# Layer 0 of a four-layer graph network: aggregate then project, or project then gather by seven products

## The chip, the cores and the metric

The kernel runs on one core of a Trainium2 chip. A core has a matrix engine (TensorE, called PE in the profile, with PEld for its weight loads), a vector engine (DVE), a scalar engine (ACT), a general engine (GpSimd, called POOL) and a queue engine (SyncE, called SP) that here issues every DMA. They run side by side and wait for each other through semaphores. The working memory is SBUF, matrix products land in PSUM. The metric is the time of one execution on the device in microseconds (us), as a median of several runs; lower is better.

## The reference

There are 64 graphs (B) of 256 nodes (N) with 512 features (F) and a dense 256x256 adjacency each. Four layers follow one another, each of the form x = x + layer(relu(layernorm(x)), adj). All is float32.

```
h = max(layernorm(x), 0)
# layer 0: attention
Wh = h @ W
e  = leaky_relu(Wh @ a[:512] + (Wh @ a[512:]).T, 0.2)
att = softmax(where(adj > 0.5, e, -9e15), axis=1)      # over the rows
x = x + elu(att @ Wh)
# layer 1: x += relu(dh * (adj + I) * dh @ h @ K1 + bias)
# layer 2: x += relu((adj @ h) @ K2) * mask
# layer 3: x += relu(concat(h, adj @ h / deg) @ W3.T)
```

Layer 0 is where the change lies: att @ (h @ W) can be computed in either order, and the logits Wh @ a need either Wh or the vectors W @ a.

## The kernel before, in words

**Tiles.** A graph's x is one tile `xs` of 128 partitions with two halves of 256 nodes, held from its load to its store. `aT` is the transposed adjacency, `h0` to `h3` are the normalised inputs of the layers, and `e` is the attention of layer 0.

**Products.** A 256x512 by 512x512 product, or a 256x256 by 256x512 one, is split into two by two blocks and done by Winograd's scheme with seven block products rather than eight (`project`, L528). It needs sums of the left blocks (S1 to S4) and of the right blocks (T1, T2, T3, T4N). Three PSUM banks `pz`, `pv`, `py` gather the products; each block is copied out ("snap") or added when its bank is ready, so that a bank is copied between two accumulations into it. `Weighted` (L491) gives the operands for x times a weight: each product has two chunks of 128 in the inner dimension, so 14 matmuls of 128x256. `Gathered` (L506) gives those for adjacency times a feature tile `y`: the inner dimension is one chunk, so 7 matmuls. A weight's blocks and their sums lie in `wb`, and `weight_sums` (L268) forms the sums on POOL.

**Two orders of a layer.** Layers 0 and 1 aggregate first: `aggregate` (L467) multiplies h by the attention or adjacency with 8 plain matmuls of 128x256, its result comes out transposed as the left operand of the projection, and `left_sums` (L453) copies it out of PSUM and forms the left sums. Layers 2 and 3 project first: `turn` (L614) transposes h in 32x32 blocks on DVE, stores it to DRAM as `hd`, loads it back as `hw` by four DMAs that complete the transposition, and forms the left sums on DVE and POOL; `neighbours` (L646) projects into a tile `y`, whose seven blocks get their right sums by `differences` (L257, two on DVE and one on POOL); `block_sums` (L665) forms the left sums of the adjacency on POOL; then a `Gathered` product follows.

**Layer 0 before.** `logit_weights` (L285) computes W a once, broadcast over the partitions, as `wa`. For each graph four DVE instructions (L711) multiply h by `wa` and sum, which gives the logits `lg`. The first set of them is needed along the free dimension: `along` (L363) does this by a DVE transposition, a store and a broadcasting load (in graphs 0 to 2 PE does it). Then ACT forms the leaky sum, DVE masks it and takes the maximum, ACT exponentiates and scales. From graph 2 on, the layer aggregates with e and then projects. Graphs 0 and 1 (`FIRST`) transpose h on PE, project first, and gather with four matmuls of 128x512 (L792), so that the projection does not wait for e.

**What sets the order.** The kernel lists all operations of all graphs with an estimated duration, and a planner in the kernel (`Plan.place`, L74) sorts them into one fixed order for each engine: at each step it takes, for every engine, the operation that can start first, and prefers those with an earlier due time (a graph's due time is 18 us after that of the graph before). Buffers are handed out by this planner too, by tag: a tile waits until one of its tag's buffers is free. The estimates are multiplied by a factor per engine (`STRETCH`, L28), and an operation of PE counts as ready only `SPARE` us (L29) after its inputs. The number of buffers for each tag stands in `buffers` (L910). The chip then follows the order with semaphores.

Of the kernel before, what the change touches and what calls it, by code (L numbers as in the profile page):

```python
# [14 lines left out]
P = 128  # L15
# [10 lines left out]
LAST, LATE = 3, 0.5  # L26

STRETCH = {"DVE": 1.15, "ACT": 1.1, "POOL": 1.1, "PE": 1.0, "DMA": 1.0}  # L28
SPARE = 0.3  # L29
# [124 lines left out]
def kernel(  # L154
# [88 lines left out]
    wa = const.tile([P, 2, F], F32, name="wa")  # L243
    wb = [const.tile([P, 7, FH, OH], F32, name=f"wb{n}") for n in range(5)]

    def spread(to, col):

        nc.tensor.transpose(to, col.to_broadcast([P, P]), ident)
# [23 lines left out]
    def weight(n, w):  # L272

        me = Tiles(f"w{n}", 0.0)
        for at, i, j in ((B11, 0, 0), (B12, 0, 1), (B22, 1, 1), (B21, 1, 0)):
            block = w[i * FH * P : (i + 1) * FH * P, j * OH : (j + 1) * OH].rearrange(
                "(k p) o -> p k o", p=P
            )
            me.op("DMA", 256, lambda g, at=at, block=block: nc.sync.dma_start(
                wb[n][:, at], block), (), [f"=wb{n}.{at}"])  # L280
        if n == 0:
            logit_weights(me)
        weight_sums(me.op, n)

    def logit_weights(me):  # L285
# [28 lines left out]
        for j in range(2):  # L314
            declare(f"pwa{j}", [P, F], "ps")
            for i in range(OC):
                op("PE", 0.9, lambda g, i=i, j=j: nc.tensor.matmul(  # L317
                    g[f"pwa{j}"],
                    lhsT=g["a_cols"][:, j * OC + i : j * OC + i + 1].to_broadcast([P, P]),
                    rhs=g[f"wt{i}"],  # L320
                    start=i == 0,
                    stop=i == OC - 1,
                ), ["a_cols", f"wt{i}"] + ([f"pwa{j}"] if i else []), [f"pwa{j}"])
            op("ACT", 0.59, lambda g, j=j: nc.scalar.copy(wa[:, j, :], g[f"pwa{j}"]),  # L324
               [f"pwa{j}"], [f"=wa{j}"])
# [32 lines left out]
    def graph(b):  # L358
# [147 lines left out]
        class Gathered:  # L506
# [14 lines left out]
            def right(self, g, at, k):  # L521
                return g[self.y][:, at]
# [5 lines left out]
        def project(operands, l, keep, keep_us, total, last, also=[], places=None):  # L528
# [8 lines left out]
            for t in "zyv":  # L537
                declare(f"p{t}{l}", [P, OH], "ps")
# [107 lines left out]
        def neighbours(l, w, by=None):  # L646
# [3 lines left out]
            declare(y, [P, 7, OH], tag="xw")  # L650
# [10 lines left out]
            project([Weighted(f"hw{l}", w)], f"y{l}", keep, 0.38, total, last, also, places=places)  # L661
            differences(op, [("DVE", 0.7), ("DVE", 0.48), ("POOL", 0.9)], lambda g: g[y],
                        lambda i: f"{y}.{i}", dict(urgent=True))

        def block_sums(l, a):  # L665
# [5 lines left out]
                g[aw][:, 0], block(g, 0, 1), block(g, 1, 1), ALU.add), [a, f"h{l}.0"], [f"{aw}.{S1}"])  # L671
# [35 lines left out]
        declare("lg", [P, 2, NC])  # L707
        declare("e", [P, NC, N], tag="mva")
        for j in range(2):
            for c in range(NC):  # L710
                op("DVE", 0.77, lambda g, j=j, c=c: nc.vector.scalar_tensor_tensor(  # L711
                    g["e"].rearrange("p c n -> p (c n)"), g["h0"][:, c, :], 1.0, wa[:, j, :], ALU.mult, ALU.mult,
                    accum_out=g["lg"][:, j, c : c + 1]),
                   [f"h0.{c}", f"=wa{j}"], ["e.0", "e.1", f"lg.{j}{c}"])
        if b < ON_PE:
            declare("pl", [P, N], "ps")
            op("PE", 0.23, lambda g: [
                spread(g["pl"][:, c * P : (c + 1) * P], g["lg"][:, 0, c : c + 1]) for c in range(NC)
            ], ["lg.00", "lg.01", "=ident"], ["pl"])
        else:  # L720
            along("pl", lambda g: g["lg"][:, 0, :], ["lg.00", "lg.01"])
        for c in range(NC):
            op("ACT", 0.47, lambda g, c=c: nc.scalar.activation(
                g["e"][:, c, :], g["pl"], AF.Prelu, bias=g["lg"][:, 1, c : c + 1], alpha=ALPHA),
               ["pl", f"lg.1{c}"], [f"e.{c}"], urgent=True)
# [38 lines left out]
        if b < FIRST:  # L764

            for half in range(2):
                pt = f"pt0_{half}"
                declare(pt, [P, FH, N], "ps")

                def go(g, half=half, pt=pt):  # L770
                    for k in range(FH):
                        for c in range(NC):
                            f0 = (half * FH + k) * P
                            nc.tensor.transpose(
                                g[pt][:, k, c * P : (c + 1) * P], g["h0"][:, c, f0 : f0 + P], ident)

                op("PE", 0.5, go, ["h0.0", "h0.1", "=ident"], [pt])
            together("pt0_0", "pt0_1")
            left_sums("pt0_0", "pt0_1", "xw0")
            declare("wh", [P, NC, O], tag="h")  # L780
            places = {(i, j): (lambda g, i=i, j=j: quarter(g["wh"], i, j), f"wh.{i}{j}")
                      for i, j in PLACE}
            project([Weighted("xw0", 0)], 0, plain_keep, 0.38, plain_total,
                    lambda pz: op("ACT", 0.38, lambda g: nc.scalar.copy(quarter(g["wh"], 1, 0), g[pz]),
                                  [pz], ["wh.10"], urgent=True), places=places)
            for i, piece in ((1, second), (0, third)):
                po = f"po{i}"
                declare(po, [P, O], "ps")

                def go(g, i=i, po=po):  # L790
                    for c in range(NC):
                        nc.tensor.matmul(  # L792
                            g[po],
                            lhsT=g["e"][:, c, i * P : (i + 1) * P],
                            rhs=g["wh"][:, c, :],
                            start=c == 0,
                            stop=c == NC - 1,
                        )

                op("PE", 1.73, go, ["e", "wh.00", "wh.01", "wh.10", "wh.11"], [po])  # L800
                elu0(i, piece[1], lambda g, po=po: g[po], [po],
                     lambda g, i=i: g["xs"][:, i, :], XS[2 * i : 2 * i + 2], O, piece[-1], "ac"[i])
            op("POOL", 0.15, lambda g: nc.gpsimd.memset(g["total1"][:, 1:2], 0.0), (), ["total1.10"])
        else:
            aggregate("h0", "e", 0)
            project([Weighted("xw0", 0)], 0, plain_keep, 0.38, plain_total, lambda _: elu0(*first, "a"))
            elu0(*second, "b")
            elu0(*third, "c")
# [99 lines left out]
    for b in range(B):  # L908
        graph(b)
    buffers = dict(  # L910
        xs=8, a_nat=1, ab=1, aT=7, h=4, mva=5, xw=5, c=2, off=1, junk=1, ex256=2, ex512=2,
        a_rows=1, a_cols=1, turned=1, row=16, hd=8, pl=1, ps=8,
    )
    for tag in ("stats", "total", "mv", "rstd", "nb", "deg", "dh", "rdeg", "lg", "top", "den", "mask"):
        buffers[tag] = 6
# [34 lines left out]
```

## Time and profile before

| | |
|---|---|
| median of 3 runs | 2808.23 us (2808.17 to 2810.1) |
| profiled execution, its own time | 2810.17 us |
| its span, first to last instruction | 2808.4 us |
| PE busy | 2785.2 us, 99% |
| DVE, ACT, POOL busy | 78%, 62%, 47% |
| DMA, mean busy share of 16 engines | 37.0% (its main queue) |

The span lies 1.8 us below the time of the same execution and equals the median to 0.2 us. A busy share is an average over the span. In the groups of instructions, a line shows the busy time, the mean of one instruction and the idle time of the engine just before, with what ended it. Matmuls overlap, so their cost is the distance between their starts rather than the duration shown for one. A float32 matmul appears as two instructions.

### The profile page before, as it was taken

What the parts mean: (1) busy time and instruction counts of PE and PEld (TensorE: products, weight loads), DVE (VectorE), ACT (ScalarE), POOL (GpSimd) and SP (SyncE); (2) the same over time, 40 slices, a digit from 0 to 9 for tenths busy, and PEclk for the clock granted to TensorE, in tenths of its full rate; (3) what the DMA queues carried; (4) which work ended last, traced back from release to release, by engine and by line L of the source; (5) the groups of instructions that cost most, each with busy time, mean ns of one, the idle gap of its engine ahead of it and who ended that gap; (6) DMA issues with size and microseconds to landing.
All of it is one profiled execution on the core that took longest, in us unless ns stands there. A gap on an engine that the chain in (4) does not pass through costs nothing.

```text
span 2808.4 us, 42034 instructions
## 1 busy us (share of the span) xinstructions
PE 2785.2 (99%) x12871; PEld 2439.3 (87%) x12871; DVE 2178.9 (78%) x5367; ACT 1750.9 (62%) x4182; POOL 1332.2 (47%) x2328
## 2 busy tenths in 40 slices
PE   7999999999999999999999999999999999999999
PEld 5888888888888888888888888888888888888887
DVE  7887787787778777877877787778777787778764
ACT  6766665666666666656666666666566666666553
POOL 6654544545444445444454444545444545444442
PEclk9999999999999999999999999999999999999999
DMA  5334433334334243333343343434334433334132
GB/s 178 72 83 97 102 87 85 87 86 96 78 88 108 73 96 98 81 88 87 88 99 75 93 96 80 102 81 96 74 96 91 94 81 94 87 81 89 53 90 69
DMA packets 752044, 251.20 MB, mean 89 GB/s; under 512 B 674756, under 2 KB 702028, under 8 KB 751820
## 3 DMA queue, kind: packets, MB, share of 16 engines
q1 hardware_dynamic: 751820, 248.52, 37.0%
q8 instruction: 103, 1.69, 0.3%
q14 instruction: 121, 0.99, 0.1%
HBM read 147.72 MB, written 100.73 MB: 88 GB/s over the span
## 4 chain that ended last, share of the span: by engine, by line
PE 98%; ACT 0%; DVE 0%; DMA 0%; POOL 0%; SPq 0%; issue 0%; DVEq 0%; ACTq 0%
PE pz L546 31%; PE pzy L546 16%; PE pv L546 16%; PE pt L477 15%; PE pvy L546 8%; PE py L546 8%; PE pyy L546 4%; PE po L792 0%; PE pwa_w L317 0%; DMA a_rows_w<-in_L_gnn_a_dram 0%; DMA wb<-in_L_gnn_kernel_dram 0%; POOL wb L264 0%; ACT h L417 0%; ACT h L438 0%; DVE e L711 0%
## 5 line engine op out<-in xcount | busy, mean ns | idle before, releaser
L546 PE MATMUL pzy<-wb,hw 128*128 128x256 f32 x2048 | 519.5, 379 | 0.0
L546 PE MATMUL pz<-wb,xw 128*128 128x256 f32 x2048 | 513.0, 379 | 1.9 <-ACT wh L585 1.3
L546 PEld LDWEIGHTS pz<-wb,xw 128*128 128x128 f32 x2048 | 387.6, 190 | 56.8 <-POOL wb L264 2.0
L546 PEld LDWEIGHTS pzy<-wb,hw 128*128 128x128 f32 x2048 | 389.1, 190 | 52.9
L438 ACT ACTIVATE h<-xs,nb,rstd 128x512 f32<-128x512 f32 x512 | 401.6, 807 | 28.8 <-POOL nb L435 23.9
L417 ACT ACTIVATE h<-xs,mv 128x512 f32<-128x512 f32 x384 | 274.9, 717 | 18.6 <-POOL mv L414 10.6
L448 POOL TENSOR_TENSOR hw<-hw 128x512 f32<-128x512 f32 x128 | 180.6, 1411 | 201.9 <-DVE hw L444 132.9
L546 PE MATMUL pz<-wb,hw 128*128 128x256 f32 x1024 | 263.0, 379 | 0.6 <-ACT c L640 0.6
L546 PE MATMUL pvy<-wb,hw 128*128 128x256 f32 x1024 | 261.0, 379 | 0.0
L546 PE MATMUL pv<-wb,xw 128*128 128x256 f32 x1024 | 258.6, 379 | 1.7 <-DVE wh L587 1.7
L836 DVE SCALAR_TENSOR_TENSOR xs<-c,xs 128x512 f32<-128x512 f32 (+1 forms) x384 | 238.4, 623 | 6.0
L477 PE MATMUL pt<-ahT,h 128*128 128x256 f32 x1024 | 233.7, 379 | 1.5 <-ACT xw L457 1.5
L477 PE MATMUL pt<-e,h 128*128 128x256 f32 x992 | 227.6, 379 | 2.3 <-ACT e L744 2.3
L448 POOL TENSOR_TENSOR xw<-xw 128x512 f32<-128x512 f32 x128 | 171.6, 1341 | 113.5 <-DVE xw L444 58.4
L477 PEld LDWEIGHTS pt<-ahT,h 128*128 128x128 f32 x1024 | 194.5, 190 | 28.7 <-issue 2.1
L546 PEld LDWEIGHTS pv<-wb,xw 128*128 128x128 f32 x1024 | 194.3, 190 | 28.5 <-DVE wh L587 2.1
L546 PEld LDWEIGHTS pz<-wb,hw 128*128 128x128 f32 x1024 | 194.4, 190 | 27.6 <-ACT c L640 1.2
L546 PEld LDWEIGHTS pvy<-wb,hw 128*128 128x128 f32 x1024 | 194.6, 190 | 26.4
L425 POOL TENSOR_TENSOR rstd<-rstd,minus_half 128x2 f32<-128x2 f32 x256 | 204.2, 797 | 19.8
L711 DVE SCALAR_TENSOR_TENSOR e<-h,wa 128x512 f32<-128x512 f32 x256 | 207.8, 812 | 7.0 <-ACT wa L324 4.5
L477 PEld LDWEIGHTS pt<-e,h 128*128 128x128 f32 x992 | 188.3, 190 | 28.2 <-ACT e L744 2.6
L414 POOL TENSOR_SCALAR mv<-total 128x1 f32<-128x1 f32 x192 | 63.8, 333 | 310.5 <-DVE xs L836 194.9
(136 smaller groups left out, 5758.5 us busy)
## 6 DMA issues: line engine op xcount, KB each, us to landing
hd<-h SPq DMA_DIRECT2D x128, 512.0 KB
hw<-hd SPq DMA_DIRECT2D x512, 128.0 KB
xs<-in_x_dram SPq DMA_DIRECT2D x64, 512.0 KB
out_dram<-xs SPq DMA_DIRECT2D x64, 512.0 KB
ab<-in_adj_dram SPq DMA_DIRECT2D x256, 64.0 KB
a_nat<-in_adj_dram SPq DMA_DIRECT2D x64, 256.0 KB
pl<-dpl SPq DMA_DIRECT2D x61, 128.0 KB
wb<-in_L_gnn_kernel_dram SPq DMA_DIRECT2D x8, 256.0 KB
```

Source lines behind the costliest of these rows:

```text
L414: op("POOL", 0.3, lambda g: nc.gpsimd.tensor_scalar(g[mv][:, 0, 0:1], g[t][:, 0:1], -1.0 / F, None, ALU.mult), [f"{t}.0"], [f"{mv}.m0"])
L417: op("ACT", 1.0, lambda g, c=c: nc.scalar.activation(g[h][:, c, :], g["xs"][:, c, :], AF.Square, bias=g[mv][:, 0, c : c + 1], accum_out=g[ ...
L425: op("POOL", 0.72, lambda g: nc.gpsimd.tensor_tensor(g[rs], g[rs], minus_half, ALU.pow), [rs, "=half"], [rs])
L438: op("ACT", 0.81, lambda g, c=c: nc.scalar.activation(g[h][:, c, :], g["xs"][:, c, :], AF.Relu, bias=g[nb][:, c : c + 1], scale=g[rs][:, c ...
L448: op("POOL", 1.45, lambda g: nc.gpsimd.tensor_tensor(flat(g[xw][:, S4 : S3 + 1]), flat(g[xw][:, A12 : A22 + 1 : A22 - A12]), flat(g[xw][:, ...
L477: nc.tensor.matmul(g[pt][:, kk, :], lhsT=g[h][:, c, k * P : (k + 1) * P], rhs=g[moving][:, c, :], start=(c == 0), stop=(c == NC - 1),)
L546: nc.tensor.matmul(g[t], lhsT=o.left(g, left, k), rhs=o.right(g, right, k), start=start and n == 0, stop=n == len(parts) - 1, skip_group_c ...
L711: op("DVE", 0.77, lambda g, j=j, c=c: nc.vector.scalar_tensor_tensor(g["e"].rearrange("p c n -> p (c n)"), g["h0"][:, c, :], 1.0, wa[:, j, ...
L836: lambda g, kw: nc.vector.scalar_tensor_tensor(to(g), y(g), 0.0, to(g), ALU.max, ALU.add, **kw), y_keys, to_keys,
```

## The change

- Layer 0 now has the form of layers 2 and 3: from graph 2 on, h0 goes through `turn(0)`; graphs 0 and 1 still transpose on PE. Then `neighbours(0, 0)` projects into `y0`, `block_sums(0, "e")` forms the left sums of the attention, and a `Gathered` product follows, in all graphs.
- W's blocks have one more column, W a: in the blocks of the left column of W it is W a[:512], in the right ones W a[512:]. The projection then gives the logits as column 257 of y0's blocks, so its matmuls are 128x257. The four DVE sums and `wa` go. `logit_weights` forms W a by 16 matmuls with two columns each, and four ACT copies put it into `wb0`, before `weight_sums`.
- The right operands y have a tag of their own with 3 buffers. Other buffers: aT 7 to 6, h 4 to 3, xw 5 to 3, c 2 to 3, ex256 2 to 3, ex512 2 to 1.
- The planner's numbers change: DVE 1.15 to 1.1, ACT 1.1 to 1.03, POOL 1.1 to 1.25, SPARE 0.3 to 0.15, and the last 2 graphs rather than 3 come due closer to one another.

```diff
-LAST, LATE = 3, 0.5
-STRETCH = {"DVE": 1.15, "ACT": 1.1, "POOL": 1.1, "PE": 1.0, "DMA": 1.0}
-SPARE = 0.3
+LAST, LATE = 2, 0.5
+STRETCH = {"DVE": 1.1, "ACT": 1.03, "POOL": 1.25, "PE": 1.0, "DMA": 1.0}
+SPARE = 0.15
...
-    wa = const.tile([P, 2, F], F32, name="wa")
-    wb = [const.tile([P, 7, FH, OH], F32, name=f"wb{n}") for n in range(5)]
+    wb = [const.tile([P, 7, FH, OH + (n == 0)], F32, name=f"wb{n}") for n in range(5)]
...
+        declare("pwa", [P, FC, 2], "ps")
+
+        def go(g):
+            for k in range(FC):
+                for i in range(OC):
+                    nc.tensor.matmul(
+                        g["pwa"][:, k, :],
+                        lhsT=g[f"wt{i}"][:, k * P : (k + 1) * P],
+                        rhs=g["a_cols"][:, i::OC],
+                        start=i == 0,
+                        stop=i == OC - 1,
+                    )
+
+        op("PE", 2.5, go, ["a_cols"] + [f"wt{i}" for i in range(OC)], ["pwa"])
+        for (half, j), at in blocks.items():
+            op("ACT", 0.2, lambda g, half=half, j=j, at=at: nc.scalar.copy(
+                wb[0][:, at, :, OH], g["pwa"][:, half * FH : (half + 1) * FH, j]),
+               ["pwa"], [f"=wb0.{at}"])
...
-            declare(y, [P, 7, OH], tag="xw")
+            declare(y, [P, 7, width], tag="y")
...
-        for j in range(2):
-            for c in range(NC):
-                op("DVE", 0.77, lambda g, j=j, c=c: nc.vector.scalar_tensor_tensor(
-                    g["e"].rearrange("p c n -> p (c n)"), g["h0"][:, c, :], 1.0, wa[:, j, :], ALU.mult, ALU.mult,
-                    accum_out=g["lg"][:, j, c : c + 1]),
-                   [f"h0.{c}", f"=wa{j}"], ["e.0", "e.1", f"lg.{j}{c}"])
+        if b < FIRST:
...
+            left_sums("pt0_0", "pt0_1", "xw0")
+        else:
+            turn(0)
+        neighbours(0, 0, x="xw0" if b < FIRST else None, width=OH + 1)
+
+        L1 = lambda g: g["y0"][:, B11 : B21 + 1 : B21 - B11, OH]
...
-            along("pl", lambda g: g["lg"][:, 0, :], ["lg.00", "lg.01"])
+            along("pl", L1, L1_KEYS)
...
-        else:
-            aggregate("h0", "e", 0)
-            project([Weighted("xw0", 0)], 0, plain_keep, 0.38, plain_total, lambda _: elu0(*first, "a"))
-            elu0(*second, "b")
-            elu0(*third, "c")
+        block_sums(0, "e")
+        project([Gathered("e", "aw0", "y0")], 0, plain_keep, 0.38, plain_total, lambda _: elu0(*first, "a"))
+        elu0(*second, "b")
+        elu0(*third, "c")
...
-        xs=8, a_nat=1, ab=1, aT=7, h=4, mva=5, xw=5, c=2, off=1, junk=1, ex256=2, ex512=2,
-        a_rows=1, a_cols=1, turned=1, row=16, hd=8, pl=1, ps=8,
+        xs=8, a_nat=1, ab=1, aT=6, h=3, mva=5, xw=3, c=3, off=1, junk=1, ex256=3, ex512=1,
+        a_rows=1, a_cols=1, turned=1, row=16, hd=8, y=3, pl=1, ps=8,
```

## The prediction, made before the changed kernel had run

> **What bounds the kernel now.** I read first the shares of the page, then the busy time of each engine in three stretches (start, middle, end), then the waits of PE alone, then the groups of instructions that the change touches.
>
> ```profile
> PE 2785.2 (99%) x12871; PEld 2439.3 (87%) x12871; DVE 2178.9 (78%) x5367; ACT 1750.9 (62%) x4182; POOL 1332.2 (47%) x2328
> 0.00:100.00 100.00, 82.50 (x354) 62.29 (x355) 79.45 (x190) 68.23 (x171) 65.54 (x92) 1.00 0.51 144
> 100.00:2790.00 2690.00, 2690.00 (x12463) 2366.50 (x12462) 2093.34 (x5166) 1679.82 (x4006) 1265.97 (x2236) 1.00 0.37 88
> 2790.00:2808.00 18.00, 12.66 (x58) 10.49 (x56) 6.13 (x12) 2.84 (x6) 0.72 (x1) 1.00 0.15 58
> ```
>
> PE is busy for 2690.0 of the 2690 us in the middle. All its idle time, 23.2 us, is 17.5 at the start and 5.3 at the end (plus rounding). So the span is PE's instructions plus those 23 us, and other engines matter only where they make PE wait. Its waits say what the start hangs on: weights from DMA, and e.
>
> ```profile
> PE pw_w L308 <- DMA wb<-in_L_gnn_W_dram: 6.5, 2, 3.8
> PE pt L477 <- ACT e L744: 2.3, 1, 2.3
> 49.61 3.45 PE pt L477 x16
> ```
>
> The last line, of the chain that ended last, gives the price of a product: 16 instructions in 3.45 us are 0.2156 us each. A float32 matmul is two of them, so 128x256 costs 0.431 us (the 379 ns of the groups includes the overlapped drain).
>
> SP, which issues every DMA in order, already stands long in places (total us, times, longest):
>
> ```profile
> SPq L623 <- DVE h L619: 440.4, 92, 19.0
> SPq L628 <- DMA hd<-h: 104.7, 42, 4.7
> ```
>
> The groups that go or are copied (busy us, mean ns, idle before):
>
> ```profile
> L711 DVE SCALAR_TENSOR_TENSOR e<-h,wa 128x512 f32<-128x512 f32 x256 | 207.8, 812 | 7.0 <-ACT wa L324 4.5
> L619 DVE STREAM_TRANSPOSE h<-h 128x512 f32<-128x512 f32 x256 | 173.6, 695 | 11.3 <-ACT h L438 11.3
> L448 POOL TENSOR_TENSOR hw<-hw 128x512 f32<-128x512 f32 x128 | 180.6, 1411 | 201.9 <-DVE hw L444 132.9 <-PE pt L477 22.4 <-PE pz L546 20.4
> L317 PE MATMUL pwa_w<-wt_w,a_cols_w 128*128 128x512 f32 x16 | 9.4, 728 | 0.0
> q1 hardware_dynamic: 751820, 248.52, 37.0%
> ```
>
> **What the Trainium skill says.** "TensorE: Matmul & The Clock Gate", section Back-to-back issue gap: N/2.4 + 2.5 ns, 215.7 ns for 512 columns. Here a 256-column float32 instruction takes 215.6 ns, so it streams 512 steps; one column more should be two steps, 0.83 ns. "SBUF — State Buffer", section Who interferes with whom: a DVE instruction with two SBUF inputs and a GpSimd instruction that reads SBUF exclude each other, while PE and ACT wait on nobody. The trace agrees: L444 takes 601 ns on xw but 449 ns on hw, the same size. "DMA: Bandwidth & Descriptors", Specifications: line rate needs 512 B or more; here 674,756 of 752,044 packets are smaller, and a turn adds such packets.
>
> **The change on PE.** Layer 0 of a graph is now 8 products of 128x256 (aggregate) and 14 (project), 22. Changed: 14 of 128x257 and 7 of 128x256. The changed order shows just this, so the change does what it says. Saved: one product, 431 ns; added: 14 x 2 x 0.83 = 23 ns; net 0.408 us. Graphs 0 and 1 swap four 512-wide products (worth 8) for 7, the same sum. 64 x 0.408 = 26.1 us. All of this is on the engine that sets the end.
> The logit weights: 16 instructions at about 0.43 us (6.9) become 32 with two columns each, bound by their weight load. The nearest rows are the transposes L344 (10 in 1.25 less drain, 0.11 each): 3.5 us. Bounds: 0.025 (the floor for small N in the same page and section) to 0.19 (a weight load), 0.8 to 6.1 us. Saved 3.4 (0.8 to 6.1). PE's work: 2785.2 - 26.1 - 3.4 = 2755.7.
>
> **What moves to other engines, per graph (from graph 2 on).** DVE loses four logit sums (4 x 0.893 with the accumulator's 81 ns) and two left sums (0.42 + 0.60), 4.59; gains two transposes (1.39), two sums of hw (0.97), three totals (1.26), two differences (0.72 + 0.49), 4.83. Net +0.2 on 34.0. ACT: -0.59 - 0.37 + 4 x 0.37 = +0.5. POOL: -1.34 + 1.41 + 0.79 (difference) + 1.78 (block sums) = +2.6 on 20.8, so 54%. At 43.1 us of PE per graph none becomes the bound (DVE about 80%). I cost these at nothing because PE's 43 us hide them; without that cover DVE's 0.2 us would still be only 15 us in all.
> DMA: one store and four loads more per graph, 4096 packets of 128 B and some 256 large ones on 11,750: by packets 37% becomes about 51%. SP: 0.34 + 4 x 0.68 = 3.1 us more of issue per graph, in one queue with inputs, outputs and the logits' row.
>
> **Does PE stay fed?** I added 0.2156 us per instruction along the changed PE order, graphs 12 to 55. From the last z product of y0 to the first product that reads e lie at least 34 us of PE work. The work needed: copy 0.37, transpose 0.23, store to load 2.25, landing at most 6.1 (load at 1199.48, Prelu at 1205.57), Prelu 1.0, minimum 0.81, maximum 0.67, exponentials 1.4, reciprocal 0.15, scaling 1.0, hops about 2: some 16. From layer 0's last z product to layer 1's first: at least 19.4 (before 23.7), needed some 10. From layer 1 to layer 2's first: at least 29.8 (before 37.1), needed some 20: norm and transposes 9, store 4.4 (issued 1180.59, loads 1184.95), loads 2.8 and landing, sums. Buffers: aT 7 to 6; from an aT's last product to the product that needs the next one in its place lie at least 44 us (before 65). So all long waits are covered, with less cover than before. Short ones are tighter: accumulations whose bank is copied between two products have at least three matmuls (1.29 us) between them; 21 pairs stand at this least distance before, 99 after. Needed: 0.21 (PE to ACT, seen at 1196.57), 0.47, 0.2 back, 0.9. A 0.81 us normalisation started just ahead can exceed it by 0.4. I allow 2 us in all for them.
>
> **The start.** Column 257 of W must be there before POOL forms W's sums; before, POOL began at 9.7 us, as soon as W had landed. Now: PE transposes W, four copies (2.4), products (3.5), four small copies (0.8), sums 2.4 + 1.4 + 1.4, done near 21 us. The first projection ends near 25 instead of 32.6, since PE no longer spends 9.4 us on pwa. But then e(0) needs y0 and graph 0's gather stands behind w3's transposes, whose load (SP) is queued behind the store hd(0 of graph 2), itself waiting for h. I get e at 34, w3 at 37, gather done at 41. Graph 2 comes through a turn, with DMA busy 57 to 99% in every 5 us until 50 here: hw near 44. Layer 1 of graph 0 starts near 55 instead of 49.5, with 23 us idle by then, and 25 in all: 7.5 more than now. Bounds: 0 (the turn lands early) and 18.
>
> **Sum.** 2755.7 + 25 + 5.3 + 2 = 2788 against the profile's span of 2808.4. The median is 2808.23, so the span stands for it: 2788, 0.7% faster.
>
> **Rivals.** (A, 0.68) the above, own range 2775 to 2800.
> (B, 0.14) short waits: 99/44 = 2.25 tight pairs a graph, each late by 0.1 us on average, add 14 us: 2802. For it: the smaller margins; against it: no wait of PE at all after 100 us today, with 21 such pairs.
> (C, 0.10) slower: hw of layer 0 lands late. Place: SP issues in order, and stands in waits of up to 19.0 us already (for the transposed h); five more transfers join it. PE stands still at the first product of y0, and every later product with it. Price: 1 us per graph is 62 us; at 0.32 us per graph the gain is gone, above 0.42 it is measurably slower; at 0.7 us, 2831. Against it: x is loaded graphs ahead.
> (D, 0.05) rows of 1028 B cost PE more than 0.83 ns: 21 products x 64 of this kind, so 15 ns each (3.5%) would eat the gain: about 2808. No 257-wide or unaligned operand is in this trace. A gain from it is excluded, since no operand became narrower; I take 0.
> The rest (0.03) is unforeseen, at any of the three.
>
> **How the numbers follow.** Faster: all of A, 0.10 of B, 0.01 of the rest and D: 0.79. Same, within 0.2% (2802.6 to 2813.8; less than that this measurement can't tell): 0.04 of B, 0.03 of D, 0.01: 0.08. Slower: C and what is left, 0.13. The range 2772 to 2811 holds A and B, and most of D; C lies above.
>
> **What would show it.** Right: PE busy near 2756 us; no idle from about 110 us to the last 20; idle of the first 100 us near 25; groups of 128x257 with a mean at most 2 ns above 379; POOL near 54%, DMA near 51%. Wrong: idle of PE spread over the middle, ended by ACT or DVE (B), or by DVE's hw or POOL's hw at y0 (C); fewer PE instructions per us than 4.64 without idle (D); or a start that costs over 18 us more.

## The result, and the profile after

The kernel after takes 2790.0 us (median of 4 runs, 2789.43 to 2790.91); the kernel before took 2808.78 us beside it on the same chip. The ratio is 0.9933, with a 95% interval of 0.9916 to 0.995: 0.7% faster. The profiled execution took 2790.29 us, its span is 2788.5 us, so spans can be set against spans: 2808.4 became 2788.5, 19.9 us less.

The shares of the page and the main DMA queue, kernel after:

```profile
PE 2766.1 (99%) x12775; PEld 2423.6 (87%) x12775; DVE 2217.1 (80%) x5305; ACT 1782.1 (64%) x4318; POOL 1464.1 (53%) x2582
q1 hardware_dynamic: 1018668, 313.56, 48.1%
```

PE has 96 instructions less: 124 fewer in the 62 graphs that aggregated first (22 products became 21), 12 more in the first two, 16 more for W a. Its busy time fell by 19.1 us and its idle time from 23.2 to 22.4 us. POOL went from 47 to 53% and DMA from 37.0 to 48.1%.

The busy time in three stretches, kernel after (the columns are the stretch, its length, then busy us and instructions of PE, PEld, DVE, ACT and POOL, the granted clock, the DMA share and GB/s):

```profile
0.00:100.00 100.00, 84.49 (x369) 69.53 (x370) 74.33 (x172) 63.41 (x173) 66.24 (x97) 0.97 0.76 186
100.00:2770.00 2670.00, 2668.78 (x12351) 2343.47 (x12350) 2136.44 (x5122) 1715.81 (x4141) 1397.10 (x2485) 1.00 0.48 111
2770.00:2789.00 19.00, 12.82 (x59) 10.62 (x57) 6.33 (x13) 2.84 (x6) 0.73 (x1) 0.92 0.15 55
```

The middle is full: 1.2 us of idle in 2670. The other idle time is 15.5 us in the first 100 (17.5 before) and 5.7 at the end (the last stretch ends 0.5 us after the span). The waits of PE over the whole span, the four largest (total us, times, longest); all but 1.2 us of its waiting before the end lies in the first 100 us:

```profile
PE pw_w L307 <- DMA wb<-in_L_gnn_W_dram: 4.4, 3, 3.7
PE pzy L551 <- ACT y L590: 3.3, 5, 1.3
PE pzy L551 <- DMA hw<-hd: 2.2, 1, 2.2
PE pt L482 <- POOL y L263: 2.0, 1, 2.0
```

The load of the transposed h, `hw`, which the change adds to layer 0, makes PE wait once, in graph 2, for 2.2 us, and never again. The same products as 128x256 and as 128x257, from the groups of instructions by shape (busy us, mean ns of one, idle before):

```profile
L551 PE MATMUL pzy<-wb,hw 128*128 128x256 f32 x2048 | 524.8, 379 | 0.5 <-ACT y L590 0.5
L551 PE MATMUL pzy<-wb,hw 128*128 128x257 f32 x992 | 256.6, 381 | 2.2 <-DMA hw<-hd 2.2
```

**The price of a graph.** In the chain of work the order of PE repeats, and so gives an exact period. Before, six graphs take 259.01 us (from 770.44 to 1029.46 us of its chain): 43.17 us each, 100 products of 0.4317. After, 16 graphs lie between these two lines:

```profile
774.88 3.45 PE pt L482 x16
...
1459.24 3.45 PE pt L482 x16
```

684.36 us by 16 is 42.77 us. A graph gained 0.396 us, 64 graphs 25.3 us. The span gained only 19.9. W a gave 2 us more (8.9 us from start to start before, 7.0 now), and idle time fell by 0.8 us, which makes 28. So about 8 us were given back, in PE's busy time; most of them can be seen at the start.

The order in time on PE in the first 68 us, kernel after (start, duration, line, tiles, count, idle before and what ended it):

```profile
10.22 6.99 PE L318 MATMUL pwa_w<-a_cols_w,wt_w 128*128 128x2 f32 x32 [0.26 <-ACT a_cols_w L295]
...
20.60 1.92 PE L551 MATMUL pzy<-wb,xw 128*128 128x257 f32 x4
22.31 1.92 PE L551 MATMUL pyy<-wb,xw 128*128 128x257 f32 x4
...
25.18 1.03 PE L551 MATMUL pzy<-wb,xw 128*128 128x257 f32 x4
...
48.35 1.94 PE L551 MATMUL pzy<-wb,hw 128*128 128x257 f32 x4 [2.20 <-DMA hw<-hd]
...
61.82 5.38 PE L482 MATMUL pt<-ahT,h 128*128 128x256 f32 x16 [2.01 <-POOL y L263]
```

Four instructions of a product take 1.03 us at 25.18, but 1.92 at 20.60 and 22.31 and 1.94 at 48.35; sixteen take 5.38 us at 61.82 instead of 3.62. PE ran at half its rate there, for about 3.4 us each time. From start to start: 20.60 to 24.02 is 1.7 us more than eight instructions of 0.2156, 48.35 to 51.79 again 1.7, 61.82 to 67.03 is 1.8 more than sixteen, and the eight transposes from 18.35 to 20.60 lose about 0.9: 6.1 us of the 8. The kernel before has no such stretch after its logit weights. The other 2 us were not placed.

### The profile page after: what moved, and what is told of

Read it like the earlier page. It is cut to its first block, busy times and chain, and to the rows that moved or that the text cites. A ratio compares the mean times of both kernels' runs of the same rounds, so it can differ in the third digit from the quotient of the medians.

```text
span 2788.5 us, 43020 instructions
## 1 busy us (share of the span) xinstructions
PE 2766.1 (99%) x12775; PEld 2423.6 (87%) x12775; DVE 2217.1 (80%) x5305; ACT 1782.1 (64%) x4318; POOL 1464.1 (53%) x2582
## 3 DMA queue, kind: packets, MB, share of 16 engines
q1 hardware_dynamic: 1018668, 313.56, 48.1%
## 4 chain that ended last, share of the span: by engine, by line
PE 98%; DVE 1%; DMA 0%; SPq 0%; ACT 0%; issue 0%; POOL 0%; DVEq 0%; POOLq 0%; ACTq 0%
PE pz L551 28%; PE pzy L551 24%; PE pv L551 14%; PE pvy L551 12%; PE pt L482 8%; PE py L551 7%; PE pyy L551 6%; PE pwa_w L318 0%; DMA a_rows_w<-in_L_gnn_a_dram 0%; DMA w3n_w<-in_L_gnn_W_dram 0%; DVE e L752 0%; DVE y L263 0%; DVE h L624 0%; SPq L691 0%; DVE y L592 0%
## 5 line engine op out<-in xcount | busy, mean ns | idle before, releaser
L551 PE MATMUL pzy<-wb,hw 128*128 128x257 f32 (+1 forms) x3040 | 772.0, 380 | 2.7 <-DMA hw<-hd 2.2
L551 PE MATMUL pvy<-wb,hw 128*128 128x256 f32 (+1 forms) x1520 | 382.6, 380 | 0.0
L590 ACT COPY y<-pzy 128x256 f32<-128x256 f32 (+1 forms) x512 | 190.7, 372 | 281.7 <-PE pzy L551 232.7
L624 DVE STREAM_TRANSPOSE h<-h 128x512 f32<-128x512 f32 x380 | 257.3, 693 | 36.0 <-ACT h L443 36.0
L551 PE MATMUL pz<-wb,xw 128*128 128x256 f32 x1024 | 263.0, 379 | 0.8 <-DVE c L804 0.5
L263 DVE TENSOR_TENSOR y<-y 128x256 f32<-128x256 f32 (+1 forms) x384 | 231.3, 628 | 7.0
L551 PE MATMUL pz<-y,aw 128*128 128x256 f32 x768 | 228.4, 379 | 0.0
L551 PE MATMUL pv<-y,aw 128*128 128x256 f32 x768 | 228.4, 379 | 0.0
L816 DVE SCALAR_TENSOR_TENSOR xs<-c,xs 128x256 f32<-128x256 f32 (+1 forms) x384 | 221.3, 578 | 3.8
L551 PEld LDWEIGHTS pz<-wb,xw 128*128 128x128 f32 x1024 | 194.0, 190 | 28.5 <-POOL rstd L426 0.9
```

Source lines behind the costliest of these rows:

```text
L263: op(eng, us, lambda g, on=on, to=to, i=i, j=j: on.tensor_tensor(tile(g)[:, to], tile(g)[:, i], tile(g)[:, j], ALU.subtract), [key(n) for ...
L551: nc.tensor.matmul(g[t], lhsT=o.left(g, left, k), rhs=o.right(g, right, k), start=start and n == 0, stop=n == len(parts) - 1, skip_group_c ...
L590: return "ACT", lambda g, to, block: nc.scalar.copy(to, block)
L624: op("DVE", 0.71, lambda g, c=c: nc.vector.transpose(g[h][:, c, :], g[h][:, c, :]), [f"{h}.{c}"], [f"{h}.{c}"])
L816: lambda g, kw: nc.vector.scalar_tensor_tensor(to(g), y(g), 0.0, to(g), ALU.max, ALU.add, **kw), y_keys, to_keys,
```

## The experiments

The theory (T): PE sets the time, a product costs 0.4317 us wherever it stands, and everything that was moved to DVE, ACT, POOL, SP and DMA is hidden. The rivals: short waits at the tight accumulations (B), the turn of layer 0 late (C), the wide rows dear (D), and, since the change has more parts than the new layer 0, that the planner's numbers or the buffers carry the gain. The runs are numbered in their order; e3 was a first form of e7.

One reading serves for all runs. Where PE's order is fixed and every instruction costs the same, lost time shows as missing instructions in a stretch, whether PE stood idle or ran at half rate. The table counts PE's instructions by stretch from the busy time of the engines, and multiplies what is missing by 0.2156 us. Runs e1 and e4 contain 128 more and 16 fewer instructions than after, which is added (27.6 us) or taken off (3.4 us). The last two rows have the kernel before as their base.

| run | 0 to 100 | 100 to 400 | 400 to 2400 | 2400 to 2700 | missing | makes | span longer by |
|---|---|---|---|---|---|---|---|
| after | 369 | 1380 | 9260 | 1391 | | | |
| e1, a product more | 372 | 1345 | 9260 | 1383 | 40 | 8.6 + 27.6 | 36.3 |
| e4, logits on DVE | 329 | 1340 | 9108 | 1359 | 264 | 56.9 - 3.4 | 53.2 |
| e5, DVE + 4 | 339 | 1334 | 9194 | 1379 | 154 | 33.2 | 32.8 |
| e6, DVE + 2 | 351 | 1360 | 9259 | 1390 | 40 | 8.6 | 8.7 |
| e8, planner back | 345 | 1338 | 9254 | 1376 | 87 | 18.8 | 18.3 |
| e10, y in xw | 369 | 1376 | 9260 | 1390 | 5 | 1.1 | 1.0 |
| e11, warm start (without its 20) | 373 | 1380 | 9260 | 1390 | -3 | -0.6 | -0.9 |
| e12, twin turn | 315 | 1376 | 9232 | 1382 | 95 | 20.5 | 20.2 |
| before | 354 | 1392 | 9268 | 1390 | | | |
| e9, before, new numbers | 299 | 1352 | 9268 | 1392 | 93 | 20.1 | 19.8 |

The last two columns agree within 0.5 us in every row, so no loss is hidden after 2700 us and each is placed. Most of it lies in the first 400 us, save in e4 and e5, where the middle loses the most or nearly as much as the start.

### A product more (e1), and wider rows (e2)

```diff
 # e1: project(), first of the seven products
+            if any(isinstance(o, Gathered) for o in operands) and l == 0:
+                product("z", A11, B11, True)
             product("z", A11, B11, True)
 # e2
-    wb = [const.tile([P, 7, FH, OH + (n == 0)], F32, name=f"wb{n}") for n in range(5)]
+    wb = [const.tile([P, 7, FH, OH + 16 * (n == 0)], F32, name=f"wb{n}") for n in range(5)]
...
-        neighbours(0, 0, x="xw0" if b < FIRST else None, width=OH + 1)
+        neighbours(0, 0, x="xw0" if b < FIRST else None, width=OH + 16)
```

> The kernel after, with one redundant product in layer 0 of each graph (the first product of the gather is formed twice, its bank started anew, so that the values stay the same): one 128x256 float32 matmul more per graph, on PE alone. Theory T (PE sets the time, a product costs 0.4317 us, the other engines are hidden): the steady period of a graph goes from 42.77 to 43.20 us, +27.6 us in all, about 2817 to 2818 us. Rival S (from the halved steps on, something beside PE sets the pace, so that PE has slack): +0 to 15 us.

> The kernel after, with 16 extra columns in place of one in layer 0's projection (all hold W a, so the work that counts is the same): 14 matmuls per graph of 128x272 instead of 128x257. Three prices of a column: linear, 0.83 ns per column and instruction, +350 ns per graph, period 43.12 us, about +22 us; the 1.3 ns that the period after shows for column 257, +550 ns, period 43.32, about +35 us; a fixed cost of an odd width or of rows that are not a multiple of 512 B (rival D), period 42.8 to 43.1, that is +0 to 22 us, or less than linear.

**Measured.** e1: 2827.75 us, ratio to before 1.0068 (1.0045 to 1.0091). e2: 2810.87 us, 1.0008 (0.9998 to 1.0019). The chain of e1, three graphs apart:

```profile
702.77 3.45 PE pt L482 x16
...
832.38 3.45 PE pt L482 x16
```

129.61 us by 3 is 43.20 us: one product is worth 0.431 us per graph, as T has it. The total missed T's number by 10 us; the table shows where: 35 instructions are missing between 100 and 400 us and 8 near the end. The planner, given one more product, made an order that loses more there.

e2's chain has 689.73 us for 16 graphs (781.03 to 1470.76): 43.11 us, 336 ns above after. By 15 columns and 28 instructions that is 0.80 ns per column, the linear price, and the whole predicts 21.5 us where the span grew by 20.9. Its group of wide instructions:

```profile
L551 PE MATMUL pzy<-wb,hw 128*128 128x272 f32 x992 | 267.9, 393 | 0.6 <-DMA hw<-hd 0.6
```

**What follows.** Rival S (PE has slack) falls, and so does rival D at the size that would matter: column 257 costs about 1.2 ns an instruction (42.773 less 99 times 0.4317, by 28), of which 0.8 is the column. What the other 0.4 is was not tried.

### The logits back on DVE (e4), and DVE loaded without another order (e5, e6)

```diff
 # e4: layer 0 keeps the new order, products 256 wide
+        for j in range(2):
+            for c in range(NC):
+                op("DVE", 0.77, lambda g, j=j, c=c: nc.vector.scalar_tensor_tensor(
+                    g["sc"], g["h0"][:, c, :], 1.0, wa[:, j, :], ALU.mult, ALU.mult,
+                    accum_out=g["lg"][:, j, c : c + 1]),
+                   [f"h0.{c}", f"=wa{j}"], ["sc", f"lg.{j}{c}"])
...
-        xs=8, a_nat=1, ab=1, aT=6, h=3, mva=5, xw=3, c=3, off=1, junk=1, ex256=3, ex512=1,
+        xs=8, a_nat=1, ab=1, aT=6, h=3, mva=5, xw=3, c=2, off=1, junk=1, ex256=2, ex512=1,
 # e5: two ahead of the mask, one ahead of each transposition of h0;
 # e6: one ahead of the mask, one ahead of one transposition
+    def dead_work(of, n):
+        for _ in range(n):
+            nc.vector.scalar_tensor_tensor(
+                dead, of, 1.0, of, ALU.mult, ALU.mult, accum_out=dead_sum)
```

> The kernel after in its order (project, then gather by seven products), but with the logits as before: four DVE sums of h0 and wa, products 256 wide, W a broadcast by 16 matmuls of 128x512; buffers c and ex256 2 instead of 3. It tells the column from the reordering. Theory T: the reordering alone gives the gain; PE work per graph 42.74 us (99 products of 0.4317), 0.03 us less than after, DVE 3.6 us more per graph (88%), hidden; W a 7 to 9 us on PE; so 2786 to 2794. Rival: without the column DVE's load makes PE wait, idle in the middle, 2800 or more; or the column is what gains, and the period goes back towards 43.17 us.

> The kernel after in its own order and with its own buffers, but each graph has four more DVE instructions that do no useful work (a 128x512 product and sum into a tile that nothing reads): two right before the mask of layer 0, one before each transposition of h0. DVE gets 3.6 us more per graph (four of 0.893 us), as the logit sums cost it, so about 88% busy; the planner does not know of them. The run with DVE logits took 2844 us with many waits of PE of about 0.4 us on copies out of PSUM. If DVE's load is their cause (theory L): PE shows such waits here too, tens of us in all, and the time is 2815 to 2850. If its planned order or its two smaller buffers were the cause (rival O): 2790 to 2796, no idle of PE in the middle.

> As the run with four idle DVE instructions per graph, but with two (one before the mask, one before one of the transpositions; 1.8 us per graph, DVE about 84%). Theory L, a smooth one: a third to a half of the loss of four. Theory L with a threshold: 2790 to 2796 here and the loss only with four. Rival O: 2790 to 2796 in both.

**Measured.** e4: 2844.33 us, 1.0124 (1.0094 to 1.0153), slower than before. e5: 2824.34 us, 1.0054 (1.0032 to 1.0077). e6: 2798.94 us, 0.9966 (0.9951 to 0.9982). The expectation T of e4 failed by 50 us. The stretch from 400 to 2400 us, first of e6, then of e5:

```profile
400.00:2400.00 2000.00, 2000.00 (x9259) 1757.17 (x9258) 1676.13 (x4070) 1296.53 (x3133) 1070.77 (x1875) 1.00 0.50 115
```

```profile
400.00:2400.00 2000.00, 1991.21 (x9194) 1743.05 (x9193) 1742.88 (x4237) 1286.76 (x3111) 1070.76 (x1864) 1.00 0.50 115
```

With DVE busy for 1676 of 2000 us (83.8%) PE loses nothing here; with 1743 (87.1%) it loses 66 instructions, 14 us. The waits of PE in that stretch, e5 and then e4:

```profile
PE pv L558 <- DVE c L655: 8.0, 12, 0.7
PE pz L558 <- DVE c L812: 0.6, 1, 0.6
```

```profile
PE pzy L546 <- ACT y L585: 10.6, 23, 0.5
PE pv L546 <- DVE c L587: 5.5, 23, 0.2
```

These are rival B's waits: a product that waits for its bank to be copied or added out. The counted idle (8.6 and 16.1 us) is less than the missing instructions (14.2 and 32.8 us); a part of each wait probably lies within the modelled ends of the matmuls. In e5 eleven of the twelve waits come 172.2 us apart, one in every four graphs. At two of them, at 1016.79 and 1189.00 us, all four added instructions stand in the 6 us ahead of the late copy, on a DVE that had not paused: at the first since 1004.89 us. In e4 ACT has a wait of its own that after has not:

```profile
ACT c L585 <- DVE xs L817: 58.2, 23, 2.5
```

Its copy into `c` waits for a `c` buffer that DVE's update of x still reads, 2.5 us every second graph, and the copies out of `pzy` stand behind it.

**What follows.** Theory L (DVE's load makes PE wait) holds. Of its two forms neither number came: e6 ends 8.9 us above after, where the threshold allowed 6 and the smooth form asked for 11 or more. In the steady state it looks like a threshold, nothing lost at 84% of DVE and 14 us at 87%; only the first 400 us lose in e6 (38 instructions, 8.2 us). But the share alone does not set it: e4 loses more than e5 at 85.6%, and e5's waits come where its added work bunches. Whether the four instructions, spread out, would cost as much was not tried. For e4 there is the second `c` buffer's loss too, and another order; those two were not separated. What is shown is that the column of logits is no ornament: this build with the seven products, the logits on DVE and one buffer fewer for `c` and for `ex256` is some 35 us slower than before.

### The turn of layer 0 (e7, e12)

```diff
 # e12: the store, and likewise the loads, issued twice, the second into DRAM that nothing reads
 # (e7: each issued twice with the same destination)
-            op("DMA", 512, lambda g: nc.sync.dma_start(
-                g[hd].rearrange("(p x) -> p x", p=P), g[h].rearrange("p c f -> p (c f)")),
+            op("DMA", 512, lambda g: [nc.sync.dma_start(
+                to.rearrange("(p x) -> p x", p=P), g[h].rearrange("p c f -> p (c f)"))
+                for to in [g[hd]] + [hd_twin] * (l == 0)],
```

> The kernel after, but layer 0's store of h and its four loads are issued twice each (5 more DMAs per graph, same data; DMA busy about 60% instead of 48%, SP 3.1 us more issue per graph). The planner does not know of them, the order is that of after. Theory T: DMA and SP have room, no idle of PE in the middle, 2790 within 4 us (the start may lose 1 to 3 us). Rival C (the turn of layer 0 is close to being late): idle of PE at the first product of y0, ended by the load of hw; 1 us per graph is 62 us, so 2820 or more.

> The kernel after, but the store and the four loads of layer 0's h are each followed by a twin with the same source, the same packets and a destination in DRAM that nothing reads, so that no twin waits for its fellow as the second loads did in the run with a doubled turn (there SP waited 626 us for the first loads to land). DMA about 60% busy, SP 3.1 us more issue per graph, order as in after. Theory T: DMA and SP have room, no idle of PE in the middle, 2788 to 2800. Rival C: hw comes late at the first product of y0, 2820 or more.

**Measured.** e7: 3451.2 us, 1.2283 (1.2248 to 1.2319). e12: 2809.46 us, 1.0002 (0.9992 to 1.0011). e3, a first form in which the planner placed the doubled transfers itself, gave no time: its order came to a point where no instruction could start. The waits of SP, which issues the DMAs, in e7:

```profile
SPq L634 <- DMA hw<-hd: 625.8, 248, 6.3
SPq L628 <- DVE h L624: 438.9, 102, 26.8
```

248 is four loads in 62 graphs. The second load writes where the first one writes, so SP stood still until the first had landed, 2.5 us each time, and every input, output and row behind it stood too. The run was meant to double the traffic and instead made SP's queue wait; it says nothing on how near after is to C, but it shows what a late turn would cost: with 10 us of such waits per graph in that queue the kernel is 661 us longer.

e12 doubles the traffic without that wait: SP shows none for `hw` any more. DMA is at 60% from 400 to 2400 us:

```profile
0.00:100.00 100.00, 76.38 (x315) 61.57 (x316) 63.38 (x148) 53.63 (x150) 54.45 (x81) 0.91 0.87 218
100.00:400.00 300.00, 298.09 (x1376) 259.79 (x1374) 243.07 (x584) 202.69 (x493) 172.02 (x299) 1.00 0.54 125
400.00:2400.00 2000.00, 1998.10 (x9232) 1750.56 (x9231) 1614.31 (x3876) 1290.31 (x3127) 1051.03 (x1872) 1.00 0.60 139
```

**What follows.** Neither theory's number came. The steady state has nearly enough room: 28 instructions, 6.0 us over 47 graphs, are lost with a second turn per graph. The start has none: with DMA at 87% in the first 100 us, 54 instructions are missing there, 11.6 us. One turn per graph, as in after, is free in the steady state (PE is busy for 2000.0 of these 2000 us there). That its loads already compete with the weights and the first inputs at the start of after is likely, with DMA at 76% there, but no run has taken the turn out.

### The planner's numbers (e8, e9), and the tag of y (e10)

```diff
 # e8: after with the first of each pair, e9: before with the second
-LAST, LATE = 3, 0.5
-STRETCH = {"DVE": 1.15, "ACT": 1.1, "POOL": 1.1, "PE": 1.0, "DMA": 1.0}
-SPARE = 0.3
+LAST, LATE = 2, 0.5
+STRETCH = {"DVE": 1.1, "ACT": 1.03, "POOL": 1.25, "PE": 1.0, "DMA": 1.0}
+SPARE = 0.15
 # e10
-            declare(y, [P, 7, width], tag="y")
+            declare(y, [P, 7, width], tag="xw")
...
-        xs=8, a_nat=1, ab=1, aT=6, h=3, mva=5, xw=3, c=3, off=1, junk=1, ex256=3, ex512=1,
-        a_rows=1, a_cols=1, turned=1, row=16, hd=8, y=3, pl=1, ps=8,
+        xs=8, a_nat=1, ab=1, aT=6, h=3, mva=5, xw=6, c=3, off=1, junk=1, ex256=3, ex512=1,
+        a_rows=1, a_cols=1, turned=1, row=16, hd=8, pl=1, ps=8,
```

> The kernel after with the planner's numbers of before (1.15, 1.1, 1.1, 0.3, the last 3 graphs closer together) and after's buffers. Theory T: the numbers decide only the order, PE has no idle in the middle either way, 2788 to 2796. Rival: the new numbers carry part of the gain; with the old ones short waits of PE come back, 2796 to 2810.

> The kernel before with only the planner's numbers of after (1.1, 1.03, 1.25, 0.15, the last 2 graphs), its buffers and its layer 0 unchanged. The steady period stays at 43.17 us a graph either way. If the numbers are good for the start by themselves (theory N): idle of PE in the first 100 us falls from 17.5, 2795 to 2805. If they only suit the new order (theory M): the start or short waits get worse, 2810 to 2830. If they are worth nothing to before: 2806 to 2811.

> The kernel after with the right operands y back in the tag of the left sums, which gets 6 buffers (3 and 3 before, so the memory is about the same). This part of the change gives no work away: if PE stays fed, the period is 42.77 us and only the start and the end can move, 2785 to 2805. Rival: y and xw then take each other's buffers and PE waits for a free one, 2810 or more, with idle in the middle.

**Measured.** e10: 2790.97 us, 0.9935 (0.9915 to 0.9955). The other two complete a square:

| | planner's numbers of before | of after |
|---|---|---|
| layer 0 of before | 2808.78 us | e9: 2829.87 us, 1.0073 (1.0053 to 1.0093) |
| layer 0 of after | e8: 2810.55 us, 1.0003 (0.9993 to 1.0013) | 2790.0 us |

The start of e8, and below it that of e9:

```profile
0.00:100.00 100.00, 77.47 (x345) 61.94 (x345) 70.52 (x156) 58.41 (x157) 61.26 (x87) 0.98 0.68 181
100.00:400.00 300.00, 294.12 (x1338) 251.23 (x1338) 236.61 (x573) 196.61 (x480) 164.39 (x289) 1.00 0.43 101
```

```profile
0.00:100.00 100.00, 74.14 (x299) 53.58 (x300) 82.20 (x183) 62.88 (x161) 63.69 (x90) 0.94 0.51 145
100.00:400.00 300.00, 296.11 (x1352) 258.84 (x1351) 226.97 (x575) 189.42 (x459) 141.12 (x252) 0.99 0.34 81
```

**What follows.** The period is 42.77 us in e8 (1172.82 to 1215.59 in its chain) and 43.17 us in e9 (701.47 to 830.98, three graphs): the price of a graph belongs to layer 0's form and not to the planner. The start depends on the planner. With the numbers of before, the new layer 0 loses 66 instructions in the first 400 us and gains nothing in all; with the numbers of after, the old layer 0 loses 95 there. Each set suits the order that it stands with. Theory M is right for e9 and the rival right for e8, though not as it was put: there are no short waits in the middle, the loss is at the two ends. The tag of y's own makes no measurable difference. Two things stay open: which of the planner's numbers it is, since all were changed together, and what the other buffer counts do. They can't carry the gain of 0.396 us a graph, since PE is full in the middle before and after, but they may have a part in the start.

### PE's clock at the start (e11)

```diff
+WARM = 10
...
+        declare("warm", [P, P], "ps")
+        op("PE", 1.5, lambda g: [
+            nc.tensor.matmul(g["warm"], lhsT=ident, rhs=ident, start=True, stop=True) for _ in range(WARM)
+        ], ["=ident"], ["warm"])
```

> The kernel after with ten idle 128x128 float32 matmuls of the identity at the head of PE's order, while PE waits for W; the order of all else is that of after. Theory K (PE's clock, still at half rate, is what made the 32 products of W a take 7.0 us and the first products of the projection 0.43 us an instruction): the transposes of W go at 0.11 us each, the 32 products take 3.5 to 5 us, the first product starts 2 to 3.5 us sooner than 20.6, and the total is 0 to 6 us less. Rival W (the 32 products are set by their weight loads or by the wait for each other): they take 7.0 us as in after, and the total is the same within 2 us, or up to 2 more.

**Measured.** 2788.76 us, 0.9928 (0.9911 to 0.9944). PE's order in time, e11:

```profile
1.34 3.93 PE L295 MATMUL warm_w<-ident 128*128 128x128 f32 x20 [1.34 <-POOL minus_half L253]
...
9.50 5.46 PE L323 MATMUL pwa_w<-a_cols_w,wt_w 128*128 128x2 f32 x32 [0.86 <-ACT a_cols_w L300]
...
18.35 1.92 PE L556 MATMUL pzy<-wb,xw 128*128 128x257 f32 x4
...
47.32 1.11 PE L556 MATMUL pzy<-wb,hw 128*128 128x257 f32 x4 [1.89 <-DMA hw<-hd]
...
60.85 3.69 PE L487 MATMUL pt<-ahT,h 128*128 128x256 f32 x16 [1.87 <-POOL y L264]
```

W a takes 5.46 us instead of 6.99 and the first product starts 2.25 us sooner; the products at 47 and 61 us run at full rate here. Some 6 us of half rate are gone (2.25, and 1.7 and 1.8 at the two places). Yet the product at 47.32 starts only 1.03 us sooner than in after, that at 60.85 only 0.97, and the end comes 0.9 us sooner.

**What follows.** Theory K is right on the cause (the 32 products of W a take about 0.11 us each as long as the clock is up, by the windows below; they come to 5.46 us, above its 3.5 to 5, because the clock falls on the way), and the total lies in its range, but a difference of 1.2 us is within what these medians can tell from nothing (the intervals of the two ratios overlap almost wholly). The order in time suggests why: the product at 47.32 still waits 1.89 us for `hw`, so what was won ahead of it is lost again to other waits. One of them is new: the next `pzy` product waits 1.50 us for ACT at 51.67, where after has no wait. At the start, half rate and idle time take each other's place.

e11 and e10 are no better than after by more than the measurement tells; no run gave a version that clearly beats it.

## Why the prediction was right, and where it was wrong

**PE is the bound and a product costs 0.4317 us: right.** e1 gives 0.431 us per graph for one product, and the middle of after is full (1.2 us idle of 2670). The saving was put at 0.408 us a graph and 26.1 us; measured 0.396 and 25.3. The term that was off is the wide column: 1.67 ns for two instructions was predicted, 2.4 came (e2: 0.80 ns per column is right, the rest was not explained). The 128x257 group's mean is 381 ns, 2 above 379.

**Side engines hidden: right in the steady state, for a reason that was only half said.** POOL 53% (54 predicted), DMA 48.1% (51), DVE 80%. The cover was taken to be PE's 43 us against DVE's 34. e5 and e6 show that the cover of DVE can end far below 100%: at 83.8% it costs nothing, at 87.1% it costs 14 us in the steady state. Rival B's tight pairs are real; e4 and e5 point to the column, which took the four logit sums off DVE, as what keeps them quiet in after. The prediction's sentence that without cover DVE's 0.2 us would be 15 us in all treated DVE's load as time in a queue. It acts as a risk of being late.

**Cover of the turn (rival C): right.** hw made PE wait once. Even a second turn per graph (e12) costs only 6.0 us over 47 graphs, 0.13 us each, less than the 0.32 at which C would have eaten the gain. At the start it costs more: e12 loses 12.5 of its 20 us in the first 400.

**The start: the sum right, its parts wrong.** Predicted were 25 us of idle time in the first 100, and W a at 3.5 us instead of 6.9. Measured: 15.5 us of idle, W a at 7.0 instead of 8.9, and 6.1 us of half rate. Most of W a before, in its order in time on PE:

```profile
11.30 1.92 PE L317 MATMUL pwa_w<-wt_w,a_cols_w 128*128 128x512 f32 x2
...
13.43 6.46 PE L317 MATMUL pwa_w<-wt_w,a_cols_w 128*128 128x512 f32 x12
```

The step that failed is the price of PE's instructions there. For W a before, 0.43 us an instruction was taken, but its first two took 1.71 us, to the next start at 13.01. For a 128x2 product, 0.11 us was taken from transposes that ran at full rate. All products were taken at 0.2156. PE's busy time came out 10.4 us above 2755.7: 1.5 for W a (3.4 saved in the prediction, 1.9 measured), 6.1 of half rate, 0.8 for the columns, and the 2 that were not placed. The idle time came out 9.9 below 32.3 (25, 5.3 and 2). That the two errors cancel to half a microsecond is luck; that they have opposite signs is not wholly. In e11 some 6 us of half rate are taken away and the total falls by 1 us, since waits take their place. The marks of the working were late too: gather done near 46 us, not 41; layer 1 of graph 0 at 61.8, not 55. Half rate does not explain that: in e11, with little of it left, layer 1 still starts at 60.85. Why was not traced.

**What the prediction left out: the planner's numbers.** It followed the changed order and so had their effect within it, but gave them no line of their own. None of its rivals was an order with a bad start, though a start over 18 us worse was among its signs of being wrong. e8 shows that this was as large a term as the saving itself: with the old numbers the same layer 0 is 20.6 us slower, and the gain is gone. e1, e8 and e9 put 7, 14 and 20 us into the first 400 us that no count of operations would give. The prediction read its start off the actual order, and so could come near it.

**The range.** 2788 us against a median of 2790.0; the likeliest case's own range, 2775 to 2800, held it.

## What to carry to other kernels

Where one engine is full, count its instructions: a change of its steady work can be priced to 1 us in 25 from one repeated distance in the chain. Price the start apart, and along the actual order, since there idle time and half rate replace each other and a planner's margins can be worth as much as the whole saving. An engine that is hidden on average can still be late where its work bunches: when work is moved onto or off it, ask what waits right behind that work, not only whether the sum fits.

## What the runs showed of the hardware that was not expected

**PE can fall to half rate while it works without a pause.** In e11 PE enters the 32 products of W a at full rate and falls out of it while it works on them without a pause. The stretches of those instructions alone (PE, PEld, granted clock, DMA share, GB/s):

```profile
9.50:10.50 1.00, 1.00 (x9) 1.00 (x10) 1.00 1.02 138
10.50:11.50 1.00, 1.00 (x10) 1.00 (x9) 0.86 0.71 72
11.50:12.50 1.00, 1.00 (x7) 1.00 (x6) 0.50 0.26 55
```

The granted clock is 1.00, 0.86 and then 0.50, and it stays there to the end of the 32. In after the same 32 products, begun at half rate, did not release it in 6.99 us. After them the first projection begins at half rate in both, e11 and after. The Trainium skill, "TensorE: Matmul & The Clock Gate", section Part 1: The HAM clock gate (the "warmup" mystery), says that the half rate is the default and that some 3.4 us of sustained activity release it; the products at 20.60 to 24.02 us of after agree if one counts from the first product (3.4 us at half rate), for the transposes ahead of it ran slow too. That section names idle time as what brings the half rate back; here PE fell back in the middle of its work. Waits of 0.48, 0.55 and 0.86 us and small transposes stand in the 3.4 us ahead of these products in e11, and may have a part; that the width of two columns is the cause was not tried. In after the granted clock of the records is 1.00 during W a, though each product takes 0.218 us, twice 0.109: the spacing of the instructions is the better witness.

**The length of a gap alone does not say whether the clock falls.** The same page, section Why this matters for your kernels, warns of gaps of more than about 3 us. In after, gaps of 2.01 and 2.20 us were followed by half rate. In before, this one of 2.33 us was not, sixteen instructions in 3.72 us (its order in time on PE):

```profile
64.36 3.72 PE L477 MATMUL pt<-e,h 128*128 128x256 f32 x16 [2.33 <-ACT e L744]
```

In e11 gaps of 1.87 and 1.89 us were not either. In e12 one of 2.21 us was followed by half rate (16 instructions in 5.38 us), and one of 2.28 us was not (four in 1.13 us). The gap of 2.20 us follows 4 us in which products alternate with small transposes and short waits, that of 2.33 us follows plain products and transposes without waits; whether this is the cause was not tried. The same page says that the window over which activity is judged runs freely, which would fit.
